# Which PSUM pool holds the transposed softmax scores in a GRU and attention kernel

## The chip, the cores and the metric

The kernel runs on one core of one Trainium2 chip. The metric is the device time of one execution in microseconds, as the median of several runs. A separate execution was recorded by the hardware profiler; all views of the profile are of that one.

The engines are named as the profile names them: PE is the matrix engine (TensorE), DVE the vector engine, ACT the scalar engine with its function tables, POOL is GpSimd, and SP issues most of the DMAs. Each takes its instructions in order and waits where an instruction depends on another engine. PSUM is the memory that PE writes its results into and that DVE and ACT can read and write; it is used in whole banks of 128 partitions by 512 numbers of 32 bits.

## The reference, cut to what matters

The model is a recommender with two recurrent passes over a history of T = 100 steps, for B = 1024 users and width 128.

```python
def gru_step(h, x_t):
    gi = x_t @ gru_Wih.T + gru_bih
    gh = h @ gru_Whh.T + gru_bhh
    i_r, i_z, i_n = jnp.split(gi, 3, axis=-1)
    h_r, h_z, h_n = jnp.split(gh, 3, axis=-1)
    r = jax.nn.sigmoid(i_r + h_r)
    z = jax.nn.sigmoid(i_z + h_z)
    n = jnp.tanh(i_n + r * h_n)
    h_new = (1.0 - z) * n + z * h
    return (h_new, h_new)
_, gru_seq = jax.lax.scan(gru_step, h0, jnp.swapaxes(item_historical_embedding, 0, 1))
keys = jnp.swapaxes(gru_seq, 0, 1)
q = jnp.broadcast_to(item_embedding[:, None, :], keys.shape)
feat = jnp.concatenate([keys, q, keys - q, q * keys], axis=-1)
score = _mlp(feat, [(att_W0, att_b0), (att_W1, att_b1), (att_W2, att_b2)], jax.nn.relu)
score = jnp.where(mask[:, :, None] == 1, score, -jnp.inf)
attn = jax.nn.softmax(score, axis=1)[..., 0]
pooled = jnp.einsum('bt,btd->bd', attn, keys)
```

A second recurrence (an attention-gated GRU) then runs over the same keys with `pooled` as its weights, and a small network gives one score for each user. The change lies in the first pass, where the softmax over the scores is formed while the GRU runs.

## The kernel before

The state is kept transposed, 128 features on the partitions and users along the free dimension, in two halves of HB = 512 users. `gru_phase` runs the loop over the steps `s`; the profile shows it from about 12 to 1396 us. The order of the work is written out by hand, and every engine keeps that order.

One step, in this order:

- Half 0 calls `gru`. Its helper `gate` makes four matmul groups at L508, each into a tile of the pool `ps`: pr (reset, from x and h), ph (from h), pi (from x) and pz (update, from x and h). Each group is cut in four column strips of 32.
- ACT makes r from pr (L520). Then `after_gate` runs the tails of earlier attention steps: `take` adds on DVE (L704), applies Relu on ACT (L709) and sends the finished row of scores to the tiles `s_b` by DMA (L716); `product` multiplies the last state with the item on DVE (L583); the loads for later steps go out on SP.
- DVE forms u from ph and r (L528) and adds it to pi (L538). ACT takes tanh of pi (L539) and sigmoid of pz (L540). DVE transposes the last state for storing (L557), forms d (L543), multiplies it with pz (L544) and adds pi, which gives the new state hn (L545). So pz is last read at L544, and pi at L545.
- After half 0 at most one waiting stage of the softmax is run (`stage`).
- Half 1 calls `gru` in the same way.
- `exponents` runs a pending Exp on ACT (L776). Sigmoid and Exp lie in different function tables, so a table load stands before Exp and another before the next sigmoid.
- `attend` makes the attention matmuls for both halves (L670) into two tiles `pm` of the pool `pa`. The third group of matmuls is the first that writes the second `pm` tile.

The history is cut in blocks, mostly of eight steps, whose ends are listed in `ENDS`. When a block's scores are complete, `softmax` queues three stages, which are run in three successive steps: `scores(0)`; `tops`, which starts with `scores(1)`; and `sums`. `scores` transposes one half's scores on DVE from `s_b` into a PSUM tile `pt` (L756) and multiplies it by the mask into `e` (L760), which is the only reader of `pt`. `pt` is made 26 times in the loop, twice for each of 13 blocks. The blocks that are finished after the loop take another tile (`banks["pt"]`).

There are two PSUM pools in this phase: `ps` with six buffers, tag "g", and `pa` with two buffers, tag "a". Every tile is one bank[...]. When a tile is asked for, the pool gives the buffer that was released first, and the first writer waits for the last users of the tile that was there. The DVE work also contains, in steps 14 to 30, a ranking of the users by length from `load_later` (for instance L385).

## Time and profile before

| | us |
|---|---|
| median of 3 runs | 2031.93 |
| lowest and highest run | 2027.62, 2031.96 |
| the profiled execution | 2054.49 |
| its span on the core | 2052.7 |

The median is the figure that the change is measured by. The profiled execution is one further run; the times of instructions below are from it, counted from the start of its span.

| engine | busy us in the window of 14 to 1396 us (1382 us) |
|---|---|
| PE | 1368.85 |
| DVE | 1258.08 |
| ACT | 527.35 |
| POOL | 1021.78 |

A row of a table of groups gives line, engine, operation, result and operands, shapes and count; then the busy time and the mean of one in ns; then the time that the engine stood idle just before such instructions, and what ended it. A row of a timeline gives start, length, engine, line and operation, and in brackets the idle time before it and its releaser. A row of waits gives who waited, for whom, the sum in us, how often, and the longest. Lines such as L508 are lines of the kernel.

### The profile page before, as it was taken

To read this page: it belongs to the slowest core of one execution; us is meant where nothing else is said; L and a number is where in the kernel's file an instruction comes from. 1 tells how busy PE (TensorE), PEld (TensorE's weight loads), DVE (VectorE), ACT (ScalarE), POOL (GpSimd) and SP (SyncE) were. 2 spreads that over 40 slices of the span, in tenths; PEclk is the share of its full clock that TensorE was granted. 3 is DMA by queue.
4 is the path that set the end of the run, shared out by engine and by line. 5 is a ranking of instruction groups with operands and counts; after the bars stand their busy time and mean duration, and the time that the engine had idled before them with its cause. 6 is when DMAs were issued, how large, how long until landed. Compare 5 with 4: busy or idle time off the path is not lost.

```text
span 2052.7 us, 41040 instructions
## 1 busy us (share of the span) xinstructions
PE 1998.8 (97%) x15452; PEld 1049.1 (51%) x15452; DVE 1763.7 (86%) x3066; ACT 824.5 (40%) x1508; POOL 1313.0 (64%) x1291
## 2 busy tenths in 40 slices
PE   8999999999999999999999999998699999999998
PEld 4655433333455544444443333334344556679997
DVE  6888999998999999989999899997377777888886
ACT  3334343333434343434343343343244444445554
POOL 0234939569797969695979787998543354443431
PEclk9999999999999999999999999999799999999999
DMA  4453233332334334333433232333432333333332
GB/s 121 97 115 105 89 105 113 96 93 78 104 113 114 108 109 124 113 99 110 135 105 100 85 99 77 102 105 103 117 101 88 94 110 98 94 102 85 93 72 37
DMA packets 241643, 205.65 MB, mean 100 GB/s; under 512 B 59270, under 2 KB 204394, under 8 KB 241434
## 3 DMA queue, kind: packets, MB, share of 16 engines
q1 hardware_dynamic: 227498, 170.43, 29.4%
q0 software_dynamic: 12352, 32.31, 5.7%
q8 instruction: 123, 2.02, 0.4%
q14 instruction: 86, 0.70, 0.1%
q10 hardware_dynamic: 1584, 0.20, 0.1%
HBM read 146.82 MB, written 54.40 MB: 98 GB/s over the span
## 4 chain that ended last, share of the span: by engine, by line
PE 83%; DVE 9%; issue 2%; DMA 2%; ACT 1%; POOL 1%; another core or an unknown queue 1%; SPq 0%; DVEq 0%; ACTq 0%; POOLq 0%
PE ps L508 42%; PE pm L670 14%; PE ph L1076 5%; PE pr L1076 4%; PE pu L1076 4%; PE pr L1072 4%; PE pu L1072 4%; PE ph L1072 4%; DVE kq L583 1%; DMA rows<-keys_d,idx_k 1%; DVE ps L538 1%; DVE d L544 1%; DVE d L543 1%; DVE u L528 1%; ACT ps L539 1%
## 5 line engine op out<-in xcount | busy, mean ns | idle before, releaser
L508 PE MATMUL ps<-x,wih 128*32 128x512 f32 x4800 | 778.3, 595 | 4.6 <-DMA x<-in_hist_x 4.0
L508 PE MATMUL ps<-hn,whh 128*32 128x512 f32 x4752 | 768.1, 592 | 0.0
L508 PEld LDWEIGHTS ps<-x,wih 128*32 128x32 f32 x4800 | 260.2, 110 | 291.0 <-issue 270.2
L508 PEld LDWEIGHTS ps<-hn,whh 128*32 128x32 f32 x4752 | 258.2, 110 | 280.1 <-issue 271.9
L539 ACT ACTIVATE ps<-ps,bih 128x512 f32<-128x512 f32 x200 | 132.4, 662 | 546.5 <-DVE ps L538 546.5
L493 POOL TENSOR_TENSOR xm<-x,m 128x512 f32<-128x512 f32 x200 | 248.1, 1240 | 121.7 <-DMA m<-mask_d 60.8
L494 POOL TENSOR_TENSOR hist<-hist,xm 128x512 f32<-128x512 f32 x200 | 269.7, 1349 | 15.7
L174 POOL DMA_INDIRECT rows<-keys_d,idx_k x220 | 213.9, 972 | 86.5 <-POOL rows L173 50.0
L607 POOL TENSOR_TENSOR pooled<-pooled,kw 128x512 f32<-128x512 f32 x191 | 257.6, 1349 | 15.0
L670 PE MATMUL pm<-hn,wk 128*32 128x512 f32 x1200 | 257.1, 592 | 4.0 <-DVE f L704 2.3
L606 POOL TENSOR_TENSOR kw<-kt,e 128x512 f32<-128x512 f32 x191 | 220.1, 1153 | 62.2 <-DVE e L779 62.1
L670 PE MATMUL pm<-kq,wkq 128*32 128x512 f32 x1200 | 257.2, 592 | 0.0
L520 ACT ACTIVATE r<-ps,brz 128x512 f32<-128x512 f32 x200 | 137.6, 688 | 285.6 <-PE ps L508 285.1
L670 PE MATMUL pm<-mv,w 128*32 128x512 f32 (+1 forms) x808 | 240.5, 592 | 8.2 <-DVE e L760 8.2
L583 DVE TENSOR_TENSOR kq<-hn,item 128x512 f32<-128x512 f32 x200 | 233.0, 1204 | 0.0
L1084 ACT ACTIVATE c<-ph,bh 128x96 f32<-128x96 f32 (+41 forms) x198 | 96.4, 487 | 292.6 <-PE ph L1076 248.3
L173 POOL COPY rows<-rest 128x1 f32<-128x1 f32 x188 | 35.3, 188 | 215.4 <-DVE rest L1113 211.7
L543 DVE TENSOR_TENSOR d<-hn,ps 128x512 f32<-128x512 f32 x198 | 136.1, 687 | 34.9 <-ACT ps L539 32.4
L1100 DVE TENSOR_TENSOR pu<-pu,c 128x96 f32<-128x96 f32 (+41 forms) x197 | 88.2, 448 | 86.0 <-ACT c L1084 77.4
L538 DVE TENSOR_TENSOR ps<-ps,u 128x512 f32<-128x512 f32 x200 | 140.0, 700 | 23.7 <-PE ps L508 3.1
L544 DVE TENSOR_TENSOR d<-ps,d 128x512 f32<-128x512 f32 x200 | 138.3, 691 | 22.7 <-ACT ps L540 3.4
L704 DVE TENSOR_TENSOR f<-pm,q 128x512 f32<-128x512 f32 x200 | 128.0, 681 | 26.5 <-PE pm L670 26.4
(180 smaller groups left out, 3101.5 us busy)
## 6 DMA issues: line engine op xcount, KB each, us to landing
x<-in_hist_x SPq DMA_DIRECT2D x212, 256.0 KB
keys_d<-kt SPq DMA_DIRECT2D x48, 1024.0 KB
m<-mask_d SPq DMA_DIRECT2D x200, 128.0 KB
rows<-keys_d,idx_k POOLq DMA_INDIRECT x220
s_b<-mv SPq DMA_DIRECT2D x200, 8.0 KB
keys_d<-kt SPq DMA_DIRECT2D x32, 64.0 KB
at<-att_d SPq DMA_DIRECT2D x34, 48.0 KB
mask_i<-in_mask SPq DMA_DIRECT2D x8, 200.0 KB
```

The source lines that it names most:

```text
L174: nc.gpsimd.indirect_dma_start(out=r[:, at, :], out_offset=None, in_=keys_d[q], in_offset=bass.IndirectOffsetOnAxis(ap=idx_k[:, k, i : i + ...
L493: nc.gpsimd.tensor_mul(d, x, m)
L494: nc.gpsimd.tensor_add(acc, acc, d)
L508: nc.tensor.matmul(p[ts(q, R), :], lhsT=w[:, g, ts(q, R)], rhs=v, start=(j == 0), stop=(j == len(parts) - 1),)
L538: nc.vector.tensor_add(pi, pi, u)
L544: nc.vector.tensor_mul(d, pz, d)
L583: nc.vector.tensor_mul(kq, h, item[:, self.cols])
L606: eng.tensor_mul(d, k, w)
L607: eng.tensor_add(acc, acc, d)
L670: nc.tensor.matmul(p[i][s, :], lhsT=w[:, s], rhs=v, start=start, stop=stop)
L1072: nc.tensor.matmul(p, lhsT=m[:, 1, :], rhs=k, start=True, stop=False)
L1076: nc.tensor.matmul(p, lhsT=m[:, 0, :], rhs=v, start=False, stop=True)
```

## The change

In the loop, the tile `pt` is taken from the pool `ps` (tag "g", six buffers) instead of the pool `pa` (tag "a", two buffers). Nothing else is edited: `pt` has the same shape, one bank, and the same writer and reader.

```diff
                 if banks:
                     pt = blocked(banks["pt"])
                 else:
-                    pt = pa.tile([P, KH, R], F32, tag="a", name="pt")
+                    pt = ps.tile([P, KH, R], F32, tag="g", name="pt")
                 nc.vector.transpose(
                     pt, s_bs[NH * (j % 2) + i].rearrange("p (k r) -> p k r", r=R)
                 )
```

In a step with a `pt`, the gates then ask for eight tiles and the scores for one, all from the six buffers of `ps`; the two buffers of `pa` serve only the two `pm` tiles of each step.

## The prediction

> **What bounds the kernel now.** I read the page first (busy shares, costliest groups), then the waits of TensorE, then the one tile that moves, then the timeline of one block where the wait on that tile costs something.

> The page and the table of groups:

> ```profile
> PE 1998.8 (97%) x15452; PEld 1049.1 (51%) x15452; DVE 1763.7 (86%) x3066; ACT 824.5 (40%) x1508; POOL 1313.0 (64%) x1291
> L508 PE MATMUL ps<-x,wih 128*32 128x512 f32 x4800 | 778.3, 595 | 4.6 <-DMA x<-in_hist_x 4.0
> L508 PE MATMUL ps<-hn,whh 128*32 128x512 f32 x4752 | 768.1, 592 | 0.0
> ```

> PE is busy nearly always, DVE not far behind. The chain of waits shows how the GRU phase (about 12 to 1396 us) goes where nothing disturbs it:

> ```profile
> 154.94 10.30 PE ps L508 x96
> 165.24 3.43 PE pm L670 x32
> 168.67 10.30 PE ps L508 x96
> ```

> One step is 128 matmul records in 10.30 + 3.43 = 13.73 us, 0.107 us each, with no hole. So in such a step only PE counts. Where does PE wait, and how does `pt` come into it?

> ```profile
> PE pm L670 <- DVE e L760: 8.2, 7, 2.1
> L756 DVE STREAM_TRANSPOSE pt<-s_b x26: 715/716/727, 162.2 to 1358.5; 128x512 f32<-128x512 f32 x26
>   DMA s_b<-mv: 2.2, 1
> ```

> The first line (waits of TensorE) says that 7 of the 26 score reads at L760 held the attention matmuls, 8.2 us in all. The others (tile `pt`) say 26 transposes, 13 blocks of two, one of which itself waited for its data. The 8.2 us are counted from the modelled end of a matmul; the lengthening of those eight steps over 13.73 us, from the starts of their matmuls in the timeline, is 10.8 us (1.07, 2.42, 1.93, 0.07, 1.32, 0.44, 3.07, 0.48). One of them, in the timeline of DVE and of PE:

> ```profile
> 275.49 0.69 DVE L544 TENSOR_TENSOR d<-ps,d 128x512 f32<-128x512 f32 x1
> 276.22 0.69 DVE L545 TENSOR_TENSOR hn<-ps,d 128x512 f32<-128x512 f32 x1
> 276.83 0.71 DVE L756 STREAM_TRANSPOSE pt<-s_b 128x512 f32<-128x512 f32 x1
> 277.57 0.29 DVE L760 TENSOR_TENSOR e<-pt,on 128x128 f32<-128x128 f32 x1
> ...
> 276.56 0.59 PE L670 MATMUL pm<-mv,w 128*32 128x512 f32 x1
> 278.01 0.59 PE L670 MATMUL pm<-mv,w 128*32 128x512 f32 x1 [0.86 <-DVE e L760]
> ```

> DVE is late here: between steps 14 and 33 it never idles for PE, having the ranking (L385, 1.27 us a step) and slow products at L583 besides. So in this stretch a wait of PE is only slack that DVE's lag forces on it. That is the reader's warning: 10.8 us of waits aren't 10.8 us to be had.

> [...] The trace has 1.283 us per load, and the activation starts 0.01 us after it, so I use 1.28 alone.

> **The change part by part.** The built instruction lists have the same instructions in the same order on every engine; only waits differ. The pool hands out the slot released first. With one tile more between the halves, eight waits move in each of the 26 steps concerned:

> 1. The second `pm` tile no longer waits for L760. This removes the waits above: at most -10.8 us.
> 2. `pz` of the second half, which waited for L528 of the first half (u), now waits for L544 of the first half (d); `pi` waits for L528 instead of the sigmoid L520; `ph`, which had no wait of its own, for L520. Order on PE: pr, ph, pi, pz (16 records), then 6 attention records, then the place of the old wait. So the new wait stands 22 x 0.107 = 2.36 us earlier in PE's queue, and everything on PE queues behind it. What releases it comes earlier too: from the end of L544 (276.18) to the end of L760 (277.86) is 1.69 us; PE followed L760 by 0.15 us, and it follows an L528 by 0.06 us in such waits. Net: a block in which both waits bind ends 2.36 - 1.69 - 0.09 = about 0.5 us later than before, not sooner.
> 3. The first tile of the next step waits for L545 and the second for L760, both some 2.5 to 4 us old by then: nothing. `pr` of the second half waits for L545 of the step before instead of L544, 0.72 us later, but its second half needed that `hn` anyway: nothing.
> 4. On ACT, the sigmoid L520 of the next step gets a second wait, on ACT itself. In the step after the second transpose that sigmoid is preceded by the table load which brings Sigmoid back after Exp. Before, the load ran at once; now the built list has wait for PE, load, sigmoid. The trace has one load that stood behind a wait already:

> ```profile
> 182.44 1.28 ACT L520 ACT_TABLE_LOAD   x1
> 184.21 0.69 ACT L520 ACTIVATE r<-ps,brz 128x512 f32<-128x512 f32 x1 [0.49 <-PE ps L508]
> ...
> 1398.71 1.28 ACT L776 ACT_TABLE_LOAD   x1 [4.50 <-DVE e L770]
> 1400.00 0.33 ACT L776 ACTIVATE e<-e 128x128 f32<-128x128 f32 x1
> ```

> So 13 loads of 1.28 us move behind `pr`. Behind them queue that sigmoid and both L709; for the sigmoid wait L528 and with it DVE's whole step.

> Now the sum, by comparing the times at which `pz` would start with the end of L544 in each of the 26 steps. Item 2 binds in steps 19, 27, 35, 36, 51, 67, 75, 76, 93, 94, 96, 97 (and by 0.09 us in 89). In 11, 12, 20, 28, 43, 44, 52, 59, 60, 68, 83, 84, 90 PE comes later than L544 by up to 1.66 us and nothing happens.
> - Steps 19 to 33: PE +0.5 at 19. In step 21 `pr` ends at 296.66 + 0.5, so the load ends near 298.5, the sigmoid near 299.2, and L528 starts some 1.15 us later than its 298.18. DVE has no idle time to take this back until step 33, so step 27 ends 1.15 + 0.5 = 1.65 us late. The load of step 29 adds as much to DVE again, but DVE's idle time at 33 and 34 (0.41 and 1.09 us) swallows what exceeds PE's delay. Together +1.65.
> - Step 35: L760 was late because the transpose waited 2.2 us for its DMA. The new wait ignores that, and PE gains some 1.8 us, but L544 of step 36 stops it 2.2 us, and at step 38 PE waits for L528 as before. 0.
> - Steps 51 and 67: holds of 0.29 and 0.25 us, of which a resumed PE makes up about 0.28 (step 19: hole of 1.34 us, step longer by 1.07). +0.2 together.
> - Steps 75, 76: +0.5. Steps 93 to 97: DVE sets the pace to the end of the phase; +0 to 0.6, I take 0.2.
> - The remaining table loads: in steps 37, 45, 53, 77, 85, 91, 95, 98 the Exp ends after `pr` is done, so the load is no later than before. In 13, 61, 69 L528 is 1.1 to 1.2 us late, PE has 4.5 to 4.8 us of slack to it, and DVE's next idle times (1.23; 0.64 and 1.27; 0.61 and 1.22) take it back. 0.
> Sum +2.55 us, taken as +2.5. The profiled execution took 2054.49 us (span 2052.7 and 1.8 around it); with the change 2057.0. The runs have a median of 2031.93, so the profile is 1.1% slower than they are; I carry the difference over unchanged: 2034.4 us, +0.12%.

> **The rivals.** About 0.3% (6.1 us) is what a measurement of this kernel can tell from no change.
> - The wait at L760 goes and nothing takes its place, or in unprofiled runs the score DMA is often late, as in step 35. For: 10.8 us of lengthened steps. Against: L544 precedes L760 by only 1.69 us on the same engine. -10.8 us: 2021. Chance 8%.
> - The table loads are carried. One mechanism: DVE has less slack than I read, each load behind `pr` delays L528 by about 1.15 us, and PE pays it at the pz that waits for L528. For: DVE is 86% busy and in steps 16, 17, 18, 27, 38 and 96 this slack is 0.06 us already. Against: in the steps right after most loads it is 1.7 to 4.8 us (0.83 and 0.47 in steps 37 and 95, where the load isn't moved). All 13 cost 15 us: 2049 with the 2.5. It decides from 4 carried loads more than my one (+2.5 + 4 x 1.15 = 7.1 us); with 8, 2044. Chance 20%.
> - Nothing is to be seen: losses of item 2 end in DVE's slack. 2032. Chance 12%, against 60% for the forecast.

> **How the numbers follow.** The forecast's own range is 2030 to 2038: bounds of 0 and +6.5 us (0.5 us for each of 13 blocks), and the 4.3 us that the three runs spread. To leave out no more than 2 in 10 I go to 2027 and 2044. Faster 0.08, same 0.72, slower 0.20.

> **What would show it.** Right: no wait of PE on L760 at L670; instead PE at L508 waits for L544 in ten or so blocks; every L520 table load idle before it on PE, and 1.28 us between the end of pr and the sigmoid; PE's undisturbed step still 13.73 us. Wrong: waits at L508 of more than 14 us in all, new waits on L528 in steps after a load (then the second rival), or no wait on L544 (then the first).

## The result and the profile after

| | before | with the change |
|---|---|---|
| median of 18 runs each, us | 2031.93 | 2036.03 |
| lowest and highest run, us | 2027.62, 2034.29 | 2032.27, 2040.62 |
| the profiled execution, us | 2054.49 | 2037.91 |
| its span on the core, us | 2052.7 | 2036.0 |
| end of the GRU phase in it (last L545), us | 1392.35 | 1398.84 |

The ratio is 1.0022 with an interval of 1.0016 to 1.0028: the change costs 4.5 us, from 3.3 to 5.7. That is less than the 0.3% named above, so it counts as no change, but with 18 runs on each side its sign is certain.

The two profiled executions can't be compared as wholes. The one with the change is 16.7 us shorter, and all of this lies behind the GRU phase: from the last L545 to the end of the span it is 660.3 us before and 637.2 after. It isn't the change. The later runs give the same kernel before 2055.90 on one chip, 2032.15 on another, and the stretch behind the GRU phase takes 661.4 us in a profile from the first chip and 637.1 in one from the second. So only the GRU phase is compared below, and there the change is 6.5 us slower in this execution (3.4 us in a second profile of the changed kernel, which is described below).

The page of the kernel with the change, its busy shares and its costliest group:

```profile
PE 1995.5 (98%) x15452; PEld 906.6 (45%) x15452; DVE 1761.8 (87%) x3066; ACT 825.8 (41%) x1508; POOL 1314.4 (65%) x1291
L508 PE MATMUL ps<-x,wih 128*32 128x512 f32 x4800 | 614.4, 596 | 17.2 <-DVE d L544 9.1
```

The idle time before L508 has gone from 4.6 to 17.2 us, and its main releaser is now L544. The chain of waits of the kernel with the change, at an undisturbed step (start, length, what):

```profile
155.18 10.30 PE ps L508 x96
165.48 3.43 PE pm L670 x32
```

It is the same 13.73 us. So nothing was lost in the steps between, and the loss must be at single places. The waits of TensorE with the change, and the tile `pt`:

```profile
PE ps L508 <- DVE d L544: 9.1, 7, 2.0
PE ps L508 <- DVE u L528: 4.1, 6, 1.2
```

```profile
L756 DVE STREAM_TRANSPOSE pt<-s_b x26: 715/716/729, 162.4 to 1365.1; 128x512 f32<-128x512 f32 x26
...
  DMA s_b<-mv: 3.6, 1
...
  PEld ps L508: 0.9, 3
```

L670 no longer waits for L760: its 8.2 us are gone. In their place PE stands at L508 for 9.1 us because of L544 and 4.1 us because of L528 (0.7 before). The transpose takes as long as it did. The last thing to see is what the table load in step 21 does. First the timeline of ACT, then that of DVE, both with the change:

```profile
296.27 0.44 ACT L776 ACTIVATE e<-e 128x288 f32<-128x288 f32 x1
298.05 1.28 ACT L520 ACT_TABLE_LOAD   x1 [1.34 <-PE ps L508]
299.35 0.69 ACT L520 ACTIVATE r<-ps,brz 128x512 f32<-128x512 f32 x1
```

```profile
298.35 0.68 DVE L583 TENSOR_TENSOR kq<-hn,item 128x512 f32<-128x512 f32 x1
300.07 0.75 DVE L528 SCALAR_TENSOR_TENSOR u<-ps,bhh,r 128x512 f32<-128x512 f32 x1 [1.04 <-ACT r L520]
```

ACT is idle for 1.34 us, waiting for `pr`, and only then loads the table. DVE has its L583 done and stands for 1.04 us until the sigmoid is there. Before, DVE never waited for that sigmoid; now it does so 7 times, 7.0 us in all:

```profile
DVE u L528 <- ACT r L520: 7.0, 7, 1.2
```

Where the 6.5 us come from, by the starts of PE's steps (with the change less before):

| from step | offset, us | what lies between it and the row above |
|---|---|---|
| 16 | +0.19 | |
| 17 | +0.88 | half 1 of step 16 held by L528 |
| 20 | +1.69 | step 19 is 1.86 us over 13.73, before 1.07 |
| 28 | +4.40 | step 27 is 5.14 us over, before 2.42 |
| 36 | +2.47 | step 35 is not longer at all, before 1.93 |
| 37 | +7.76 | step 36 is 5.28 us over, before nothing |
| 77 | +7.44 | small gains and losses |
| 97 | +8.84 | step 96 is 4.51 us over, before 3.07 |
| end | +6.49 | |

Three steps are longer than any wait in them explains. The timeline of PE in step 27, with the change:

```profile
387.37 1.07 PE L508 MATMUL ps<-x,wih 128*32 128x512 f32 x8 [1.02 <-DVE u L528]
390.44 1.79 PE L508 MATMUL ps<-x,wih 128*32 128x512 f32 x8 [2.01 <-DVE d L544]
391.99 1.95 PE L508 MATMUL ps<-hn,whh 128*32 128x512 f32 x8
```

Groups of eight matmuls that otherwise take 1.04 us take 1.79 and 1.95 us behind the second hold. The windows of the same trace say why (stretch, length, busy time of PE, PEld, DVE, ACT and POOL, then the granted clock of PE):

```profile
387.23:390.64 3.41, 1.26 (x12) 0.32 (x16) 2.99 (x6) 1.84 (x3) 1.60 (x2) 1.00 0.45 144
390.64:394.06 3.42, 3.42 (x20) 0.87 (x16) 3.28 (x6) 0.49 (x1) 3.22 (x3) 0.50 0.02 5
516.95:520.36 3.41, 1.40 (x16) 0.42 (x16) 3.09 (x6) 1.84 (x3) 3.25 (x4) 1.00 0.96 311
1346.38:1349.79 3.41, 1.22 (x12) 0.16 (x8) 3.08 (x6) 1.78 (x3) 3.33 (x3) 1.00 0.65 207
```

A hold is a time in which PE stands and waits. For 3.41 us after the second hold PE ran at half its clock. The first, third and fourth line are the windows just before the three such spans of the GRU phase, in steps 27, 36 and 96. The trace of the kernel before has no such span in that phase.

### The profile page after: what moved, and what is told of

Same layout as the page of the kernel before. It is cut to its first block, busy times and chain, and to the rows that moved or that the text cites. A ratio compares the mean times of both kernels' runs of the same rounds, so it can differ in the third digit from the quotient of the medians.

```text
span 2036.0 us, 41014 instructions
## 1 busy us (share of the span) xinstructions
PE 1995.5 (98%) x15452; PEld 906.6 (45%) x15452; DVE 1761.8 (87%) x3066; ACT 825.8 (41%) x1508; POOL 1314.4 (65%) x1291
## 4 chain that ended last, share of the span: by engine, by line
PE 74%; DVE 14%; POOL 4%; issue 4%; DMA 2%; ACT 2%; SPq 0%; DVEq 0%; ACTq 0%; POOLq 0%
PE ps L508 34%; PE pm L670 12%; PE ph L1076 5%; PE pr L1076 5%; PE pu L1076 4%; PE pu L1072 4%; PE ph L1072 4%; PE pr L1072 4%; DVE kq L583 3%; DVE ps L538 2%; DVE d L543 2%; DVE d L544 2%; DVE u L528 2%; ACT ps L539 2%; DMA rows<-keys_d,idx_k 1%
## 5 line engine op out<-in xcount | busy, mean ns | idle before, releaser
L508 PE MATMUL ps<-x,wih 128*32 128x512 f32 x4800 | 614.4, 596 | 17.2 <-DVE d L544 9.1
L508 PE MATMUL ps<-hn,whh 128*32 128x512 f32 x4752 | 605.4, 594 | 0.0
L508 PEld LDWEIGHTS ps<-x,wih 128*32 128x32 f32 x4800 | 178.3, 110 | 359.3 <-issue 252.1
L508 PEld LDWEIGHTS ps<-hn,whh 128*32 128x32 f32 x4752 | 178.2, 110 | 334.5 <-issue 295.5
L493 POOL TENSOR_TENSOR xm<-x,m 128x512 f32<-128x512 f32 x200 | 247.6, 1238 | 123.0 <-DMA m<-mask_d 62.0
L520 ACT ACTIVATE r<-ps,brz 128x512 f32<-128x512 f32 x200 | 137.8, 689 | 282.2 <-PE ps L508 281.5
L583 DVE TENSOR_TENSOR kq<-hn,item 128x512 f32<-128x512 f32 x200 | 234.1, 1209 | 0.0
L670 PE MATMUL pm<-hn,wk 128*32 128x512 f32 x1200 | 214.5, 594 | 3.3 <-ACT q L248 2.1
L670 PE MATMUL pm<-kq,wkq 128*32 128x512 f32 x1200 | 213.5, 592 | 0.0
L670 PE MATMUL pm<-mv,w 128*32 128x512 f32 (+1 forms) x808 | 196.0, 595 | 0.0
L544 DVE TENSOR_TENSOR d<-ps,d 128x512 f32<-128x512 f32 x200 | 138.3, 691 | 22.5 <-ACT ps L540 3.2
L528 DVE SCALAR_TENSOR_TENSOR u<-ps,bhh,r 128x512 f32<-128x512 f32 x198 | 146.7, 741 | 12.2 <-ACT r L520 7.0
```

What stands on the lines that cost most here:

```text
L493: nc.gpsimd.tensor_mul(d, x, m)
L508: nc.tensor.matmul(p[ts(q, R), :], lhsT=w[:, g, ts(q, R)], rhs=v, start=(j == 0), stop=(j == len(parts) - 1),)
L528: nc.vector.scalar_tensor_tensor(out=u, in0=ph, scalar=bhh[:, 2:3], in1=r, op0=ALU.add, op1=ALU.mult,)
L583: nc.vector.tensor_mul(kq, h, item[:, self.cols])
L670: nc.tensor.matmul(p[i][s, :], lhsT=w[:, s], rhs=v, start=start, stop=stop)
```

## The experiments

Three causes were on the table.

- A: the late table loads delay DVE, and PE pays for it at its next hold.
- B: the new hold of some 2 us at pz (L544), in these three steps behind one at pi (L528), brings a span of half clock.
- C: the move of the wait in itself, that is, the sum of the prediction without the loads.

The expectations call the forecast (C, and the loads at the size that it gave them) theory 1, A theory 2 and B theory 3.

Ratios are to the kernel before, run beside it on the same chip; in us they are taken of that median. The first four share one chip (before 2055.90), the next four a second (2032.15), then two a third (2030.35) and the last two again share one (2030.56).

**The change with an early load.** A sigmoid of one column behind each Exp brings the table back at once; its result isn't used.

```diff
-                nc.scalar.activation(e[:, :, :rows], e[:, :, :rows], AF.Exp)
+                nc.scalar.activation(e[:, :, :rows], e[:, :, :rows], AF.Exp); nc.scalar.activation(table, table, AF.Sigmoid)
```

> The changed kernel, with a sigmoid of one column right behind each Exp on ACT, so that the table load for Sigmoid runs at once again and no longer stands behind the wait for pr. The new bank waits stay. Theory 1 (forecast: holds +1.2 us, late loads +1.3): about 1.3 us faster than the changed kernel, +2.5 to +3 against before. Theory 2 (the loads are carried and are most of it): back to before within 1 us. Theory 3 (PE's granted clock halves for 3.4 us after a step with two holds, seen three times in the trace after, 1.7 us each): the load of step 21 makes DVE 1.2 us late, so holds in step 27 get shorter and the half-clock spans there go: 2 to 3 us faster than the changed kernel, one or two spans left.

Measured: 2057.58 us, ratio 1.0009 (1.0003 to 1.0016), +1.9 us. ACT's timeline in step 21:

```profile
295.40 1.28 ACT L776 ACT_TABLE_LOAD   x1
296.69 0.20 ACT L776 ACTIVATE table<-table 128x1 f32<-128x1 f32 x1
296.80 0.67 ACT L520 ACTIVATE r<-ps,brz 128x512 f32<-128x512 f32 x1
```

The sigmoid runs as soon as `pr` is there. DVE no longer waits for it anywhere, and the waits of PE on L528 shrink from 4.1 to 1.3 us. So the late loads, with what they bring after them, are about half of the loss: 1.0022 against 1.0009. One span of half clock is left, in step 27, which theory 3 had expected to go. The window before it:

```profile
384.66:388.07 3.41, 1.40 (x16) 0.21 (x16) 2.99 (x6) 1.84 (x3) 1.45 (x2) 1.00 0.47 149
```

PE has one hold in that step, 2.01 us for L544, and none for L528. So one hold of this length can be enough.

**The kernel before with a late load.** `pt` stays in `pa`; a copy of one column of `pr` ahead of the sigmoid makes the load wait for `pr`, as the change does. The copy's result isn't used.

```diff
+                soft.pop("late", None) and nc.scalar.copy(table, pr[:, 0:1])
                 nc.scalar.activation(r, pr, AF.Sigmoid, bias=brz[:, 0:1])
...
                 nc.scalar.activation(e[:, :, :rows], e[:, :, :rows], AF.Exp)
+                soft["late"] = True
```

> The kernel before, with a copy of one column of pr on ACT in front of the sigmoid that follows an Exp, so that the 13 table loads stand behind pr as in the changed kernel; the bank waits are those of before. The copy adds about 0.2 us to each. Theory 1: +1.2 to +1.5 us against before. Theory 2: +4 us or more. Theory 3: +1.2 us if no half-clock span appears in the GRU phase, 1.7 us more for each that does.

Measured: 2061.38 us, ratio 1.0029 (1.0018 to 1.0039), +6.0 us. First ACT's timeline in step 21, then the waits of PE:

```profile
297.61 0.16 ACT L520 COPY table<-ps 128x1 f32<-128x1 f32 x1 [1.15 <-PE ps L508]
297.77 1.28 ACT L520 ACT_TABLE_LOAD   x1
299.06 0.69 ACT L520 ACTIVATE r<-ps,brz 128x512 f32<-128x512 f32 x1
```

```profile
PE pm L670 <- DVE e L760: 10.8, 11, 2.9
```

The late load alone (with 0.16 us of copy in front of it), without any move of `pt`, costs about as much as the whole change; the intervals overlap. The wait on L760 grows from 8.2 to 10.8 us, because L760 comes late with everything else on DVE, and a half-clock span appears in step 27 here too (the mean granted clock of these runs is 0.9905, against 0.9911 before). That shows that A costs time by itself. That A costs more here than inside the change fits with step 35: here the late DMA still holds PE (3.09 us), with the change it doesn't. That this is the cause isn't shown.

**No PSUM bank for the scores at all.** `pt` goes to SBUF, so that neither pool hands out a tile for it.

```diff
-                    pt = pa.tile([P, KH, R], F32, tag="a", name="pt")
+                    pt = sp.tile([P, KH, R], F32, name="pt", bufs=1)
```

> The kernel before, with pt in SBUF (one buffer), so that no matmul waits for the score transposes at all and the table loads stay early. If the 10.8 us by which the eight steps of before are longer are only slack under a late DVE: 0 to -2 us against before. If they are to be had: -8 us or more.

Measured: 2058.84 us, ratio 1.0015 (1.0007 to 1.0023), +3.1 us: a loss, with no wait on L760 left and no late load. The tile `pt` (shortest, median and longest time in ns) and the waits of PE:

```profile
L760 DVE TENSOR_TENSOR e<-pt,on x26: 292/460/1153, 162.6 to 1361.4; 128x128 f32<-128x128 f32 x20, 128x96 f32<-128x96 f32 x2, 128x64 f32<-128x64 f32 x2, 128x48 f32<-128x48 f32 x2
...
  DMA s_b<-mv: 4.2, 1
```

```profile
PE ps L508 <- DVE u L528: 8.4, 13, 1.4
PE ps L508 <- DVE d L544: 2.5, 3, 1.2
```

Two things are to be seen. L760 takes 0.46 us in the median and up to 1.15 us, where it took 0.29 and at most 0.30 us from PSUM. And PE waits anyway: not at L760, but one ring further on, at the gates' own L528. Where DVE is behind, PE is stopped by whichever tile it needs next: 10.9 us in all, where it was 8.2 for L760 and 0.7 for L528. This speaks against the idea that the old wait on L760 was itself a cost, but it isn't a clean test. By the starts of PE's steps this kernel was 3.2 us ahead of the kernel before at step 36. It lost 5.0 us in steps 36 to 38, where a transpose waited 4.2 us for the DMA of the scores, a wait that the kernels with `pt` in PSUM have as well (2.2 us before).

**The change with filled holds.** Eight extra matmuls, whose results nobody uses, stand before the pz of half 1 in the three steps that showed half clock. They keep PE busy in its hold and change no wait.

```diff
-                pz = gate(1, both)
+                fill(x) if self.i and t in (27, 36, 96) else None; pz = gate(1, both)
...
+        def fill(x):
+            p = pa.tile([P, HB], F32, tag="a", name="fill")
+            [nc.tensor.matmul(p[ts(q % 4, R), :], lhsT=wih[:, 0, ts(q % 4, R)], rhs=x, start=True, stop=True) for q in range(8)]
```

> The changed kernel, with eight more matmuls of 32 columns (16 records, 1.7 us) into an unused pm buffer ahead of pz of the second half in steps 27, 36 and 96 alone, the three steps with two holds and a half-clock span; their results are not used. Theory 3: no half-clock span in the GRU phase of the trace, and 3 to 5 us faster than the changed kernel (about -0.2%), near +0 to +1 against before. Theories 1 and 2: the same time as the changed kernel or up to 1.7 us more for each step where the hold is shorter than the filling.

Measured: 2057.05 us, ratio 1.0009 (1.0000 to 1.0017), +1.9 us. The timeline of PE in step 27, and the windows there:

```profile
385.80 1.06 PE L508 MATMUL ps<-x,wih 128*32 128x512 f32 x8 [1.02 <-DVE u L528]
386.68 1.90 PE L812 MATMUL fill<-x,wih 128*32 128x512 f32 x16
388.87 1.06 PE L508 MATMUL ps<-x,wih 128*32 128x512 f32 x8 [0.29 <-DVE d L544]
389.76 1.04 PE L508 MATMUL ps<-hn,whh 128*32 128x512 f32 x8
```

```profile
387.00:390.40 3.40, 3.11 (x32) 0.81 (x28) 3.05 (x6) 1.49 (x3) 3.04 (x3) 1.00 0.18 64
```

With more work on PE the kernel is quicker. The hold ends when it did, but the matmuls behind it take 1.06 and 1.04 us, and there is no half clock in the phase. The three steps are 3.44, 3.60 and 2.47 us over 13.73, against 5.14, 5.28 and 4.51. The difference is 1.7, 1.7 and 2.0 us. A span of 3.41 us at half clock can cost at most half of its length, 1.7 us, so the third difference holds 0.3 us of something else. That isolates B; no other engine's work and no wait for another engine changes. In the runs the extra matmuls gain 2.2 to 2.6 us, where 3 to 5 were expected.

**The change again, on a second chip.**

> The changed kernel itself, for a ratio on the chip that the other runs of this group use. Expected +0.2% against before, as on the first chip, with two to four half-clock spans of 3.41 us in the GRU phase of its trace, at steps 27, 36 and 96.

Measured: 2036.23 us, ratio 1.0020 (1.0014 to 1.0027), +4.1 us, as in the first comparison. Its profile has half clock in steps 36 and 96 only; step 27 is 3.42 us over. The spans thus come and go between executions of one kernel. They aren't peculiar to the profiled ones: the clock granted to PE is on record for every run, over the whole execution. On this chip its mean is 0.9932 with the change and 0.9950 before, which is 3.6 us of full speed lost.

**The change with both remedies**, the early load and the filled holds.

> The changed kernel with both mends: a sigmoid of one column behind each Exp (table load early) and the eight filling matmuls in steps 27, 36 and 96. If holds, late loads and half-clock spans are the whole of the loss: 0 to +1 us against before, 3 to 4 us faster than the changed kernel, no half-clock span in these steps. If the bank waits cost more by themselves: +2 us or more is left.

Measured: 2032.59 us, ratio 1.0003 (0.9995 to 1.0011), +0.6 us. No half clock is in the GRU phase of its profile. With A and B gone nothing measurable is left against the kernel before, at most some 2 us. As a bound for C this is too low, however. The mean granted clock of these runs is 0.9959, above the 0.9950 of the kernel before, which is 1.8 us of full speed. So the kernel before runs at half clock in places too, and some of that is gone here as well. If PE was busy in all of it, C is 0.6 + 1.8, about 2.4 us, by this estimate; the sum of the prediction without the loads is 1.4.

**A thinner ranking.** If DVE's lag sets the holds, the remedy may be less DVE work in the steps around a score block rather than another bank. The ranking runs one pass in each step from 14 on; here it rests a step after each pass.

```diff
                     accum_out=rank[:, g : g + 1],
                 )
-                yield
+                yield; yield
```

On the kernel before:

> The kernel before, with a step of rest between the eight passes of the ranking (L385), so that DVE has 1.35 us of extra work in every second step only. The late DVE of steps 22 to 27 should go, and with it the 2.42 us of step 27: 1 to 3 us faster than before. If PE's waits there have another cause: no change.

On the change:

> The changed kernel with the same spreading. If DVE's lag is what makes the new waits bind and what brings the half-clock span of step 27: that span goes, step 27 is not longer than 14.5 us, and the difference to the spread kernel before shrinks to 1 to 3 us (from 4 to 5). If the new waits cost time whatever the lag: the difference stays at 4 to 5 us.

Measured: 2026.11 us, ratio 0.9972 (0.9961 to 0.9983), for the kernel before; 2028.48 us, 0.9981 (0.9971 to 0.9991), with the change. The kernel before with the ranking spread, 5.7 us quicker, beats both kernels of this case. Its waits of PE:

```profile
PE pm L670 <- DVE e L760: 2.5, 3, 1.9
```

The wait that the change set out from falls from 8.2 to 2.5 us, with `pt` where it was; steps 19, 27 and 35 are no longer lengthened at all. With the change step 27 is 14.66 us long, without half clock, where at most 14.5 was expected, and the difference to the spread kernel before is 2.4 us, as expected.

Not all of the gain is DVE work, though. In step 35 the kernel before is late because the transpose waits 2.2 us for the DMA of the scores. In all eight profiles without the spread a transpose waits for a DMA there, 2.2 to 4.3 us, and in none of the six with it. In the trace of the kernel before SP stood 16.3 us, waiting for a product on POOL (L493), with this DMA behind it in its queue; with the spread it was 1.1 us. The ranking has work on POOL too (L397), which the spread moves to later steps. So 1.93 us of the 5.7, those of step 35, seem to come by POOL and SP; no run took that part alone.

**The spread with other remedies.** The change with the spread and the early load, and the spread with `pt` in SBUF:

> The changed kernel with the ranking spread and the table load early, no filling. The spread changed kernel was 2.4 us slower than the spread kernel before. If its late loads are that difference (step 16 was 0.9 us longer in it, steps 92 and 93 3.1 us longer): within 1 us of the spread kernel before, -0.25% against before. If the holds at pz are: no better than the spread changed kernel, -0.19%.

> pt in SBUF with the ranking spread: no bank wait for scores at all, and DVE less late. If a PSUM wait for pt is worth anything once DVE is less late: faster than the spread kernel before by 1 us or more (-0.33% or better against before). If DVE's slower read of pt from SBUF (L760 at 460 ns in the middle instead of 291) eats it: slower than the spread kernel before, -0.1 to -0.25%.

Measured: 2029.87 us, ratio 0.9996 (0.9987 to 1.0004), and 2028.69 us, ratio 0.9987 (0.9979 to 0.9996). The second says that taking away the bank altogether doesn't beat leaving it in `pa`, with the ranking spread either. The first is a miss: the early load, worth 2 us elsewhere, brought nothing. Its profile has a half-clock span in step 96, and the mean granted clock of its runs is 0.9945 against 0.9953 before, 1.7 us of full speed. Two more runs, on one chip, asked whether the chip or that span is to blame; the second adds the eight extra matmuls of above in step 96.

> The change with the ranking spread over twice as many steps, once more, beside the next run on one chip. If its earlier ratio of 0.9981 belongs to the kernel, it comes again (0.997 to 0.999). If the earlier group's chip made it, as the early load with the spread (0.9996) on another chip may suggest, it lies near 0.9996 here.

> The change, the ranking spread, the early table load, and eight extra matmuls whose results nobody uses before the pz of half 1 in step 96, where the profile of the kernel without them had a span of half clock. If that span is why the early load gained nothing there, the time falls by one such span (about 1.7 us, 0.08%) from 0.9996 to about 0.9988 or below, and is no slower than the kernel without the early load beside it. If the early load itself costs something where the ranking is spread, it stays near 0.9996 and lies above its neighbour.

Measured: 2026.93 us, ratio 0.9982 (0.9975 to 0.9988), and 2028.81 us, ratio 0.9990 (0.9981 to 0.9998). The first repeats its earlier ratio, so the chip isn't to blame. Nor is a span in step 96 the whole of it: the profile of this first run has one there as well. The second lies where a removed half-clock span would put it, but still 1.9 us above its neighbour, with intervals that overlap a little. Step 46 of its profile, first the windows, then DVE:

```profile
644.78:648.19 3.41, 1.38 (x19) 0.17 (x10) 3.34 (x3) 0.25 (x1) 3.17 (x3) 1.00 0.29 91
648.19:651.60 3.41, 3.41 (x18) 0.78 (x22) 3.06 (x5) 1.84 (x3) 3.30 (x4) 0.50 0.48 152
```

```profile
644.28 3.18 DVE L583 TENSOR_TENSOR kq<-hn,item 128x512 f32<-128x512 f32 x2
```

Its neighbour, the change with the spread alone, at the same place:

```profile
645.07 2.24 DVE L583 TENSOR_TENSOR kq<-hn,item 128x512 f32<-128x512 f32 x2
```

There is half clock in step 46, where two products took 3.18 us rather than 2.24 and PE stood 2.04 us for L528 rather than 1.10. The hold isn't chance of one execution: the profile of the early load without the extra matmuls has it too, 2.05 us, and the four profiles of spread kernels without an early load have 1.10 or 1.11. So the early load costs some 0.9 us in step 46 once the ranking is spread. The half clock behind it came in one of the two profiles, and in the runs at large it doesn't explain the 1.9 us: the mean granted clock of the second is 0.9952, of the first 0.9954, about 0.3 us. What the rest is stays open.

## Why the prediction was right, and by how much it was off

- **The wait on L760 goes, and its 10.8 us aren't to be had**: right. No PE wait on L760 is left, and the wait on L544 is there, in 7 places with a visible hole, somewhat fewer than the ten or so foretold. Step 19, a step where both waits bind, was to be 0.5 us longer; it is 0.79. With `pt` in `pa` the matmuls waited for L760 because `pm` was written into the buffer from which `pt` was still read; with `pt` in `ps` this wait falls from 8.2 us to nothing.
- **Nothing from the next step's pr and ph**: right. PE has no hold for L545 in the phase.
- **Thirteen loads behind the wait for pr**: right in kind; in step 21 L528 waits 1.04 us for the sigmoid, where 1.15 were put down. Seven loads stand idle for `pr`, not all thirteen as the list of signs has it and not the five that the working leaves (21, 29, 13, 61 and 69; it missed 37 and 85). The term was too small, though: the early load takes back 0.11% to 0.13%, over 2 us (the change at 1.0022 and 1.0020, with the early load 1.0009), of which a part is half clock that DVE's delay brings on. With the holds filled the early load is worth 1.3 us (1.0009 against 1.0003, with intervals that overlap), close to the 1.15. And the second rival, carried loads, has more to it than its 20% suggest. Its first sign, waits at L508 of more than 14 us, was missed closely (13.2). Of its second, new waits on L528, there are four (0.7 to 4.1 us in all), in steps 16, 27, 36 and 96, none in the step right after a load; those of 27 and 36 go with an early load. And the kernel before with late loads alone loses 6.0 us.
- **Steps 19 to 33, +1.65**: right but for the half clock. By step 28 the profile of the change has +4.40, of which 0.9 us were there before step 19, most of it from a slow product in step 15 (1.69 us, before 0.68) that held PE in step 16; the second profile of the same kernel doesn't have it. Steps 19 to 27 add 3.5 us. Of this 1.7 are half clock, and 1.8 remain for the 1.65. In the second profile, without half clock in step 27, these steps add 1.8 too.
- **Step 35 gains 1.8 us and step 36 gives it back**: the gain is 1.93, as worked out. What it costs in step 36 was mis-sized: 2.2 us were put down, for L544, and step 36 is 5.28 us over. The hold for L544 is 2.01 us, as foretold. What the sum lacked is a hold of 1.16 us for L528 just before it and 1.7 us of half clock. DVE was later than it was taken to be: the DMA of the scores kept the transpose waiting 3.6 us and not 2.2, and two products took 3.28 us instead of 2.38 before.
- **Steps 51, 67, 75, 76: +0.7**: small, as foretold; from step 39 to step 77 the offset grows by 0.37.
- **Steps 93 to 97, DVE sets the pace**: right. The offset falls from 7.50 at step 93 to 6.49 at the end, although step 96 has a span of half clock.

So the forecast named the places and the mechanism. What it lacked is one term: it took a hold of PE to cost its own length. Here what follows a hold of 2 us may cost up to 1.7 us more. Two or three such spans are in each profile of the change; with the extra matmuls in those holds the loss is 1.9 us (0 to 3.5), which agrees with the sum of 2.5 us without that term.

## What to carry to other kernels

A wait on a lagging engine isn't removed by another buffer: ask which tile the waiting engine needs next, and whether the new wait stands earlier in its queue. Look at what a new dependency does to the things that are put before an instruction, such as a table load that ran in idle time and now stands behind a wait. And where PE is the bound, count by how much PE stands within 3.4 us, since here one hold of 2.0 us (step 27), or two of 0.69 and 1.95 us (step 96), brought 3.41 us at half clock as well. Spreading the work of the lagging engine over more steps (here one `yield`) gained more than either place for the tile.

## What the runs showed of the hardware

```profile
388.31:391.72 3.41, 1.42 (x16) 0.63 (x20) 3.24 (x7) 0.01 (x1) 3.33 (x3) 1.00 0.02 5
```

It has 1.42 us in a window and kept its clock, where windows with 1.38 to 1.46 us in other profiles were followed by half clock. So in that range it can go either way; the ends of matmuls are modelled. The grid doesn't start with the kernel: traced back to the start of the span, its first line lies at 2.57 us in the trace of the kernel before and at 1.53 us with the change. So the same hold can lie in one window in one execution and be split between two in another: step 27 is 5.14 us over in one profile of the change and 3.42 in the other, with holds of the same length (1.0 and 2.0 us). In the second PE was busy for 1.96 and 1.86 us of the two windows there, and no half clock followed.

**Products from SBUF have no fixed price.** L583, with both operands in SBUF, takes 0.67 to 2.27 us for the same shape in the kernel before, and L760 went from 0.29 to as much as 1.15 us when `pt` moved to SBUF. In the trace of the kernel before, the slow products go with work on POOL. The 45 products with no POOL instruction beside them take at most 0.68 us. Of the 200 products 131 take more than 0.7 us: each started while a POOL instruction ran, and each ended 0.55 to 0.56 us after the end of such an instruction, as if it had waited for that and then done its work. The other 24 met one and took at most 0.70 us. So a shift of DVE against POOL can change which products are slow, as in step 15, where one took 1.69 us with the change and 0.68 before, and single steps of two profiles can differ by this alone.
